# Second layer of a conv/attention hybrid: depthwise sum in PSUM, a scan whose two products add in PSUM, and its side work placed anew

## Chip, cores, metric

The kernel runs on one core of a Trainium2 chip. The metric is device time in microseconds of one whole execution (four layers). All arithmetic is float32, a few small products in float32r.

## What is computed

Only the second layer (L1) is touched. For each of 4 images (128 channels, 64x64) it does a 1x1 product, a depthwise 3x3 convolution with SiLU, a product down to 32 features, and two Mamba-2 scans over the 4096 positions, one forward and one backward; then a batch norm and a gate.

```python
def _mamba2(u, W_in, conv_w, conv_b, dt_bias, A_log, D, norm_w, W_out):
    zxbcdt = u @ W_in
    z, xBC, dt = ...                       # 64, 64+64+64, 1 columns
    xBC = silu(causal_dwconv1d(xBC, conv_w, conv_b))
    xs, Bm, Cm = ...                       # 64 columns each
    dt = softplus(dt + dt_bias)
    dA = exp(dt * -exp(A_log))
    def step(h, inp):
        h = dA_t * h + dtx_t[..., None] * B_t[:, None, :]
        return h, einsum('bhpn,bn->bhp', h, C_t)
    y = (scan of step) + D * xh
    y = y * silu(z)
    y = y * rsqrt(mean(y * y, -1) + 1e-05) * norm_w
    return y @ W_out

o = einsum('bihw,io->bohw', x, lin1_w) + lin1_b
o = silu(depthwise3x3(o, dw_w) + dw_b)
s = o @ fc_in_w
y1, y2 = _mamba2(s, ...[0]), flip(_mamba2(flip(s), ...[1]))
o = batchnorm((y1 + y2) @ fc_out_w)
x = sigmoid(conv4(o)) * x + x
```

## The kernel before, in words

`layer1` (L1007) splits each image's 4096 positions into 8 **groups** of 4 **tiles** of 128 positions; 32 groups in all. The forward and the backward scan go side by side (`dr` 0 and 1). Within a tile the scan is a product of matrices: a masked matrix of decays times C·B (`pairs`, `weigh`, `within`), plus C times the state that came into the tile (`update`).

The main loop (L1485) runs over G, and each group has four **slots** j = 0 to 3. A slot does a piece of several groups at once, in an order written out by hand: the object `InOrder` (L74) makes every engine's instructions stand in program order, so an engine's queue is what the loop says. In the slots of G stand

- for group G: `update` (PE: new state into CY columns 256:320, C times state into 128:192; then DVE: `hst` = state · decay + CY), `weigh` (DVE: `lmc` = `lm` · CY), `within` (PE: `lmc` times x into CY 192:256), `pairs` of the next tile (PE: C·B into CY 0:128), `gated` of the tile before (DVE: two scalings `y` by `ecs`, a sum with the `within` part; POOL: product with the gate into Y);
- for G+1: `spans` (POOL: `ta`), `silus` (ACT), `masks` (PE `psseg`, ACT exp into `lm`), `inputs` (POOL `xw`, DVE `xdt`), `turn_b` (PE `psb`, DVE copy into B), `skips` (ACT);
- for G+2: `project_c` (PE `psc`), `silu_c` (ACT), `lengths` (ACT and eleven small DVE operations), `sums` (PE `pscs`, DVE), `decays` (ACT, POOL);
- for G+3: `project` (PE `pstm` from S4), `take` (DVE: `tm`, `u`);
- for the group 12 ahead (`now`): the nine steps of the convolution, step 0 on ACT and steps 1 to 8 on DVE (L1144), two in each slot; one further ahead (`nxt`) `lines` (PE `pslin`, ACT `lp`); one behind (`last`) `conv_silu` (ACT) and `features` (PE `pss`, four ACT copies into the shifted rows of S4);
- `behind` (L1402): normalisation and output of groups that are done, a generator advanced one step per slot.

The convolution runs for G up to 19, that is in 20 groups that also scan; G = 20 to 31 scan alone. CY is two PSUM tiles of two banks each, used in turn by j. Four further banks (`mm`) serve all other products in turn.

Of the kernel before, what the change touches and what calls it, by code (L numbers as in the profile page):

```python
# [8 lines left out]
F32 = mybir.dt.float32  # L9
# [85 lines left out]
class Kernel:  # L95
# [911 lines left out]
    def layer1(self, after):  # L1007
# [13 lines left out]
        with ExitStack() as ctx:  # L1021
# [23 lines left out]
            def weights():  # L1045
                ps = mm("psw2")
                nc.tensor.matmul(ps[:, 0:P], out_wT, fc_out, start=True, stop=True)
                nc.vector.tensor_scalar(w2, ps[:, 0:P], self.col("norm_w"), None, ALU.mult)
                taps = gp.tile([P, 2, 192], F32, name="taps", tag="C", bufs=3)
                nc.sync.dma_start(taps, self.ins["taps4"])  # L1050
                nc.vector.tensor_mul(wx[:, :, 0:192], wx[:, :, 0:192], taps)
# [6 lines left out]
            nA = cp.tile([P, 2], F32, name="nA")  # L1058

            def constants():  # L1060
# [11 lines left out]
                nc.vector.tensor_copy(ident_r, self.ident)  # L1072
                nc.scalar.activation(nA, self.row("A_log"), AF.Exp)
                nc.vector.tensor_scalar(nA, nA, -1.0, None, ALU.mult)
# [6 lines left out]
            CY = [pp.tile([P, 2, 512], F32, name=f"CY{k}") for k in range(2)]  # L1081
# [53 lines left out]
            def conv(n, b, k):  # L1135
                lp = lps[n, b]
                if k == 0:
                    own = space(n, b)
                    co = own[1] if own else gp.tile([P, 8, HW], F32, name="co")
                    cos[n, b] = co  # L1140
                    nc.scalar.activation(co, lp[:, 0:8, 0:HW], AF.Copy, scale=dw[:, 0:1])
                    return
                co = cos[n, b]
                nc.vector.scalar_tensor_tensor(  # L1144
                    co, lp[:, k // 3:k // 3 + 8, k % 3:k % 3 + HW], dw[:, k:k + 1], co, ALU.mult, ALU.add)
# [10 lines left out]
            def conv_silu(n, b):  # L1156
                src = cos[n, b]
                if len(src.shape) == 2:
                    src = src.rearrange("p (r c) -> p r c", c=HW)
                    own = space(n, b)  # L1160
                    cos[n, b] = own[1] if own else gp.tile([P, 8, HW], F32, name="co")
                nc.scalar.activation(cos[n, b], src, AF.Silu, bias=self.col("dw_b"))

            def features(n, b, moved=False):

                s = S4[n % 2]
                if b == 0:
                    nc.gpsimd.memset(s[:, 0:3], 0.0)
                    nc.gpsimd.memset(s[:, L:L + 3], 0.0)
                ps = mm("pss")  # L1170
                nc.tensor.matmul(ps, fc_in4, cos[n, b].rearrange("p r c -> p (r c)"), start=True, stop=True)
                if moved:
                    nc.scalar.copy(cos[n, b].rearrange("p r c -> p (r c)"), ps)
                for m in range(4):
                    ms = slice(32 * m, 32 * m + 32)
                    if moved:
                        plain.sync.dma_start(s[ms, b * 512 + m:b * 512 + m + 512],
                                             cos[n, b][ms].rearrange("p r c -> p (r c)"))
                    else:
                        nc.scalar.copy(s[ms, b * 512 + m:b * 512 + m + 512], ps[ms, :])  # L1180
# [49 lines left out]
            def silu_c(g):  # L1230
                q = groups[g]
                q.C = gp.tile([P, 512], F32, name="C", bufs=3)
                nc.scalar.activation(q.C, q.pc, AF.Silu, bias=self.col("cb_C"))

            def turn_b(g):
# [5 lines left out]
                nc.vector.tensor_copy(q.B, ps)  # L1241
# [3 lines left out]
            def small(name):  # L1245
                return sp.tile(sh, F32, name=name, bufs=4)

            def lengths(g):
# [3 lines left out]
                u, e, w, lg = q.u, small("e"), small("w"), small("lg")  # L1252
# [16 lines left out]
                q.parts = small("lead"), small("rest")  # L1269
# [4 lines left out]
            def spans(g, dr):  # L1274
                q = groups[g]
                full = [P, GS, P]
                q.ta = []
                for part in q.parts:
# [3 lines left out]
                    q.ta.append(ta)  # L1282

            def sums(g):
# [8 lines left out]
                q.cs = small("cs")  # L1293
                q.tot, q.wd = small("tot"), small("wd")
# [5 lines left out]
            def decays(g):  # L1300
                q = groups[g]
                q.ecs = small("ecs")
                q.et = sp.tile([P, GS], F32, name="et", bufs=4)
                nc.scalar.activation(q.ecs, q.cs, AF.Exp)
# [23 lines left out]
            def masks(g, dr):  # L1328
# [5 lines left out]
                for k, ta in enumerate(q.ta):  # L1334
# [8 lines left out]
            def block(q, dr, j):  # L1343
                b = j if dr == 0 else GS - 1 - j
                return q.C[64 * dr:64 * dr + 64, b * P:(b + 1) * P]

            def pairs(g, j):
                q = groups[g]
                for dr in range(2):
                    nc.tensor.matmul(CY[j % 2][:, dr, 0:P], q.B[64 * dr:64 * dr + 64, j * P:(j + 1) * P],  # L1350
                                     block(q, dr, j), start=True, stop=True)
# [3 lines left out]
            def weigh(g, j):  # L1355
                q = groups[g]
                lm = kp.tile([P, 2, P], F32, name="lmc")
                nc.vector.tensor_tensor(lm, q.lm[:, :, j, :], CY[j % 2][:, :, 0:P], ALU.mult)
                weighted[g, j] = lm

            def update(g, j):
# [5 lines left out]
                cy = CY[j % 2]  # L1367
                for dr in range(2):
                    nc.tensor.matmul(cy[64 * dr:64 * dr + 64, 0, 256:320],
                                     q.tm[:, j, 128 + 64 * dr:192 + 64 * dr], q.xw[:, j, dr, :],  # L1370
                                     start=True, stop=True)
# [4 lines left out]
                nc.vector.scalar_tensor_tensor(h2, state[0], q.et[:, j:j + 1], cy[:, 0, 256:320],  # L1376
# [3 lines left out]
            def within(g, j):  # L1380
                q = groups[g]
                lm = weighted.pop((g, j))
                for dr in range(2):
                    nc.tensor.matmul(CY[j % 2][:, dr, 192:256], lm[:, dr, :], q.xdt[:, j, dr, :],
                                     start=True, stop=True)

            def gated(g, j):
                q = groups[g]
                n, i = divmod(g, NG)
                r, cy = GS * i + j, CY[j % 2]  # L1390
# [92 lines left out]
            for x in left[0:2]:  # L1483
                features(*x, True)
            for G in range(NG + 1 - AHEAD, N + 1):  # L1485
# [9 lines left out]
                if G >= 1 and i >= NG // 2:  # L1495
                    backs.append(behind(n, NG - 1 - i))
                if later:
                    dts = lengths(G + 2)

                for j in range(GS):  # L1500
                    if now is not None and j == 0:
                        conv(*now, 0)
                    if later and j == 0:
                        project_c(G + 2)
# [3 lines left out]
                    if later and j == 0:  # L1508
                        silu_c(G + 2)
                    if last is not None and j == 0:  # L1510
                        conv_silu(*last)
                    if j == 0 and (later or soon or here):
                        nc.scalar.preload_act_table_set("natural_log_exp_and_others")
                    if here:
                        if j == 0 and G == 0:
                            pairs(0, 0)
                        update(G, j)
                        weigh(G, j)
                    if 0 <= G - 1 < N and j == 0:
                        gated(G - 1, GS - 1)  # L1520
                    if here and j:
                        gated(G, j - 1)
                    if first:
                        project(G + 3, j)
                    if soon and j == 1:
                        masks(G + 1, 0)
                        spans(G + 1, 1)
                        inputs(G + 1)
                        turn_b(G + 1)
                    if soon and j == 2:  # L1530
                        masks(G + 1, 1)
                        skips(G + 1)
# [15 lines left out]
                    if nxt is not None and j == 1:  # L1548
                        lines(*nxt)
                    if last is not None and j == 2:  # L1550
# [3 lines left out]
                    for b in list(backs):  # L1554
# [1346 lines left out]
```

## Time and profile before

| | us |
|---|---|
| median of 3 runs | 4900.45 (4896.83 to 4912.55) |
| the profiled execution | 4906.88 |
| its span, first to last instruction | 4904.8 |
| busy in the span: PE / DVE / ACT / POOL | 4487.7 / 3588.3 / 3608.9 / 3064.4 |
| first and last update of the state (`hst`) | 916.1 and 1587.9 |
| update at j = 0 of group 20 | 1386.2 |

The profile writes `DVE` for VectorE, `ACT` for ScalarE, `POOL` for GpSimd, `PE` and `PEld` for TensorE's products and weight loads, `SPq` for the SyncE queue that issues DMAs. A group line reads: line, engine, operation, out<-in, shape, count, busy us, mean ns of one, idle time before and what ended it. Nearly all lines say L85, the helper that records every operation, so tiles' names tell the operations apart. In a windows line the last columns are the granted TensorE clock (1.00 is full speed), the DMA share and GB/s. A float32 product appears as two passes, so counts of PE lines are twice the program's.

### The profile page before, as it was taken

The page shows a single profiled execution, that of the slowest core. Times are in us where ns is not written, and L with a number is a line of the kernel's source. Part 1 is how long each engine was busy: PE and PEld are TensorE (multiplying, and loading weights), DVE is VectorE, ACT ScalarE, POOL GpSimd, SP SyncE. Part 2 cuts the span into 40 slices and gives each one's busy share as a digit, 9 for nine tenths or more (in the row PEclk, how much of TensorE's full clock was granted, in tenths as well). Part 3 has the DMA queues.
Part 4 walks back from the last instruction along what each step waited for, and adds up shares of the span by engine and source line. Part 5 has one row for each costly group of instructions (what it writes and reads, how often), then busy time and mean ns, then how long its engine had stood idle before and what let it go on. Part 6 is the DMA issues. An engine that isn't in the chain of part 4 may idle for free. (4 is left out here: it accounts for less than half of the span.)

```text
span 4904.8 us, 65981 instructions
## 1 busy us (share of the span) xinstructions
PE 4487.7 (91%) x22552; PEld 2439.1 (50%) x22552; DVE 3588.3 (73%) x7198; ACT 3608.9 (74%) x5496; POOL 3064.4 (62%) x3043
## 2 busy tenths in 40 slices
PE   6889977888999699997997999999999999999798
PEld 4777765566666344443443444444444444444344
DVE  5999996788876788874775666666666666665675
ACT  4466644555554677775766999999999999999575
POOL 0334443355555345552797888888888888877488
PEclk9999998788788899998999999999999999999899
DMA  6667772000000300000000000000000000000000
GB/s 211 182 187 187 199 185 67 12 9 10 18 12 16 96 5 1 1 1 0 18 35 18 1 1 1 1 1 1 1 1 1 1 1 1 1 1 1 8 28 35
DMA packets 67474, 190.47 MB, mean 39 GB/s; under 512 B 12532, under 2 KB 15796, under 8 KB 65460
## 3 DMA queue, kind: packets, MB, share of 16 engines
q1 hardware_dynamic: 61700, 170.19, 12.2%
q0 software_dynamic: 2240, 12.85, 0.9%
q8 instruction: 182, 2.98, 0.3%
q10 hardware_dynamic: 3184, 3.08, 0.2%
q14 instruction: 168, 1.38, 0.1%
HBM read 133.23 MB, written 50.74 MB: 38 GB/s over the span
## 5 line engine op out<-in xcount | busy, mean ns | idle before, releaser
L85 POOL TENSOR_TENSOR r<-r 128x512 f32<-128x512 f32 (+1 forms) x1088 | 1349.1, 1241 | 331.6 <-DVE r L85 271.4
L85 DVE TENSOR_TENSOR r<-r,num 128x1024 f32<-128x1024 f32 (+1 forms) x1088 | 974.8, 927 | 597.5 <-PE num L85 502.6
L85 PE MATMUL D<-F,G 32*128 32x512 f32 (+3 forms) x4608 | 1139.9, 573 | 1.8 <-DVE den L85 0.9
L85 PE MATMUL num<-F,G 32*128 32x512 f32 (+3 forms) x4608 | 1057.1, 590 | 6.8 <-DVE r L85 3.9
L85 ACT ACTIVATE r<-r 128x2048 f32<-128x2048 f32 (+4 forms) x610 | 1018.6, 1679 | 51.4 <-POOL r L85 4.3
L85 ACT ACTIVATE r<-D 128x1536 f32<-128x1536 f32 (+1 forms) x544 | 763.4, 1403 | 49.6 <-PE D L85 29.3
L85 PEld LDWEIGHTS D<-F,G 32*128 32x128 f32 x4608 | 484.8, 184 | 372.8 <-issue 235.2
L85 PE MATMUL acc<-r,v 128*128 128x512 f32 (+3 forms) x1152 | 598.1, 606 | 0.7 <-ACT r L85 0.7
L85 POOL TENSOR_TENSOR x<-x 128x512 f32<-128x512 f32 (+2 forms) x320 | 405.4, 1267 | 148.5 <-DVE m L85 66.3
L85 PEld LDWEIGHTS num<-F,G 32*128 32x128 f32 x4608 | 383.4, 183 | 223.4 <-issue 111.4
L85 PE MATMUL pff<-hid,w_ffn_w2T 128*128 128x512 f32 x1024 | 468.0, 600 | 0.0
L85 PE MATMUL pex<-w_expert_w,vT 128*128 128x512 f32 x1024 | 462.6, 600 | 1.6 <-DVE x L85 1.4
L85 POOL TENSOR_TENSOR piece<-v,wt 128x512 f32<-128x512 f32 x160 | 167.5, 1064 | 373.3 <-DVE cum L85 91.7
L85 PEld LDWEIGHTS acc<-r,v 128*128 128x128 f32 x1152 | 174.1, 188 | 382.7 <-issue 188.9
L85 PE MATMUL acc<-ident,pr 128*128 128x128 f32 x2560 | 322.0, 284 | 42.0 <-DVE pr L85 42.0
L85 ACT ACTIVATE x<-pex,gate 128x128 f32<-128x128 f32 x896 | 256.6, 367 | 104.0 <-PE pex L85 78.8
L85 PEld LDWEIGHTS acc<-ident,pr 128*128 128x128 f32 x2560 | 299.2, 147 | 55.8 <-DVE pr L85 54.1
L85 ACT ACTIVATE hid<-phh,cols 128x512 f32<-128x512 f32 x416 | 252.8, 688 | 67.1 <-PE phh L85 67.0
L85 PEld LDWEIGHTS pex<-w_expert_w,vT 128*128 128x128 f32 x1024 | 191.2, 193 | 217.2 <-issue 160.7
L85 PEld LDWEIGHTS pff<-hid,w_ffn_w2T 128*128 128x128 f32 x1024 | 184.9, 190 | 200.6 <-issue 200.6
L85 DVE TENSOR_TENSOR pr<-v,near_w 128x2560 f32<-128x2560 f32 x96 | 270.0, 2813 | 5.6 <-PE acc L85 4.8
L85 POOL TENSOR_TENSOR Y<-y,tm 128x64 f32<-128x64 f32 x256 | 111.7, 456 | 236.3 <-DVE y L85 149.2
(495 smaller groups left out, 7916.4 us busy)
## 6 DMA issues: line engine op xcount, KB each, us to landing
v<-tab SPq DMA_DIRECT2D x320, 256.0 KB
oms<-omw SPq DMA_DIRECT2D x32, 432.0 KB
omr<-oms SPq DMA_DIRECT2D x32, 432.0 KB
X<-in_x_dram SPq DMA_DIRECT2D x8, 1024.0 KB
tab<-vb SPq DMA_DIRECT2D x64, 128.0 KB
o<-o SPq DMA_DIRECT2D x32, 256.0 KB
oin<-o SPq DMA_DIRECT2D x32, 256.0 KB
kept<-X SPq DMA_DIRECT2D x4, 2048.0 KB
```

The costliest lines, as they stand in the source:

```text
L85: self.last = op(*args, **kwargs)
```

## The change

- The convolution's running sum stands in PSUM (`cop`), not in SBUF (`co`), outside the prologue; `conv_silu` writes it to an SBUF tile `co` that has one buffer.
- `features` copies `pss` once into `co` and sends it to S4's four shifted rows by four DMAs (this was the way of the prologue); the two last features of the prologue go by copies, two on ACT and two on DVE.
- `decay` (new): two products per direction with `half_r` give the decay to each position, ACT takes exp, POOL multiplies C by it (`Ce`). The states' product then uses `Ce`, and it and `within` add in the same PSUM columns; `gated` loses its two scalings. `ecs` is gone.
- CY is one tile of two banks; tiles j even and odd use two halves of each bank. `project_c` makes C in tile order, in eight products of 128 columns.
- The copy into B goes from DVE to ACT.
- Slots: `weigh` ahead of `update`, `gated` ahead of both; `silu_c` one group later; `project_c`, `lines`, `skips`, `features` in slot 3; the convolution's steps 3, 2, 1, 2 per slot; up to G = 27 one generator of `behind` advances per slot, not all.

```diff
             def conv(n, b, k):
-                    co = own[1] if own else gp.tile([P, 8, HW], F32, name="co")
+                    co = own[1] if own else pp.tile([P, 512], F32, name="cop").rearrange(
+                        "p (r c) -> p r c", c=HW)
...
             def conv_silu(n, b):
+                    cos[n, b] = gp.tile([P, 8, HW], F32, name="co", bufs=1)
...
-            def features(n, b, moved=False):
+            def features(n, b, moved=True):
...
-                nc.tensor.matmul(q.pc[0:64, :], wx[:, 0, 0:64], s4(g, 0, 0, 512), start=True, stop=True)
-                nc.tensor.matmul(q.pc[64:128, :], wx[:, 1, 0:64], s4(g, 1, GS - 1, 512), start=True, stop=True)
+                for j in range(GS):
+                    for dr in range(2):
+                        nc.tensor.matmul(q.pc[64 * dr:64 * dr + 64, j * P:(j + 1) * P], wx[:, dr, 0:64],
+                                         s4(g, dr, j), start=True, stop=True, skip_group_check=True)
...
-                nc.vector.tensor_copy(q.B, ps)
+                nc.scalar.copy(q.B, ps)
...
+            def decay(g, dr):
+                q = groups[g]
+                if dr == 0:
+                    q.pr = pp.tile([P, 512], F32, name="psrow")
+                for k, ta in enumerate(q.ta[dr]):
+                    nc.tensor.matmul(q.pr, half_r[:, 64 - 64 * dr:192 - 64 * dr], ta.rearrange("p j t -> p (j t)"),
+                                     start=(dr == 0 and k == 0), stop=(dr == 1 and k == 1))
+                if dr == 1:
+                    q.Ce = gp.tile([P, 512], F32, name="Ce")
+                    nc.scalar.activation(q.Ce, q.pr, AF.Exp)
+                    nc.gpsimd.tensor_tensor(q.Ce, q.Ce, q.C, ALU.mult)
...
             def update(g, j):
-                    nc.tensor.matmul(cy[:, dr, 128:192], block(q, dr, j), state[0][64 * dr:64 * dr + 64, :],
-                                     start=True, stop=True)
+                    nc.tensor.matmul(CY[:, dr, at(j, 128, 192)], block(q.Ce, dr, j),
+                                     state[0][64 * dr:64 * dr + 64, :],
+                                     start=False, stop=False, skip_group_check=True)
...
             def within(g, j):
-                    nc.tensor.matmul(CY[j % 2][:, dr, 192:256], lm[:, dr, :], q.xdt[:, j, dr, :],
-                                     start=True, stop=True)
+                    nc.tensor.matmul(CY[:, dr, at(j, 128, 192)], lm[:, dr, :], q.xdt[:, j, dr, :],
+                                     start=False, stop=True, skip_group_check=True)
...
             def gated(g, j):
-                for dr in range(2):
-                    nc.vector.scalar_tensor_tensor(y[:, dr, :], cy[:, dr, 128:192], q.ecs[:, j, dr:dr + 1],
-                                                   q.tm[:, j, 64 * dr:64 * dr + 64], ALU.mult, ALU.add)
-                nc.vector.tensor_tensor(y, y, cy[:, :, 192:256], ALU.add)
+                nc.vector.tensor_tensor(y, q.tm[:, j, 0:128].rearrange("p (d e) -> p d e", d=2),
+                                        CY[:, :, at(j, 128, 192)], ALU.add)
...
                 for j in range(GS):
+                    if last is not None and j == 0:
+                        conv_silu(*last)
                     if now is not None and j == 0:
                         conv(*now, 0)
...
                     if here:
+                        weigh(G, j)
+                        update(G, j)
...
-                    if now is not None:
-                        for k in ((1, 2), (3, 4), (5, 6), (7, 8))[j]:
-                            conv(*now, k)
+                    steps = ((1, 2, 3), (4, 5), (6,), (7, 8))[j] if now is not None else ()
...
-                    if last is not None and j == 2:
+                    if last is not None and j == (2 if last[1] == NG - 1 else 3):
                         features(*last)
...
-                    for b in list(backs):
+                    for b in backs[0:1] if one_by_one else list(backs):
```

More of the change, by code (lines that the diff above doesn't have):

```diff
@@ L1048, in weights @@
                 nc.vector.tensor_scalar(w2, ps[:, 0:P], self.col("norm_w"), None, ALU.mult)
-                taps = gp.tile([P, 2, 192], F32, name="taps", tag="C", bufs=3)
+                taps = gp.tile([P, 2, 192], F32, name="taps", tag="C")
                 nc.sync.dma_start(taps, self.ins["taps4"])
@@ L1058, in layer1 @@
             nA = cp.tile([P, 2], F32, name="nA")
+            half_r = cp.tile([P, 192], F32R, name="half_r")
             def constants():
@@ L1072, in constants @@
                 nc.vector.tensor_copy(ident_r, self.ident)
+                for k in range(3):
+                    nc.vector.tensor_scalar(half_r[:, 64 * k:64 * k + 64], late[:, 0, 0:64], 0.0,
+                                            1.0 if k == 1 else 0.0, ALU.mult, ALU.add)
                 nc.scalar.activation(nA, self.row("A_log"), AF.Exp)
@@ L1078, in layer1 @@
             Y = cp.tile([P, NT + 2 * GS, 2, DI], F32, name="Y")
-            CY = [pp.tile([P, 2, 512], F32, name=f"CY{k}") for k in range(2)]
+            CY = pp.tile([P, 2, 512], F32, name="CY")
             kept = [dram.tile([P, 512], F32, name=f"o{k}") for k in range(NB * NG)]
@@ L1157, in conv_silu @@
                 src = cos[n, b]
+                own = space(n, b)
                 if len(src.shape) == 2:
                     src = src.rearrange("p (r c) -> p r c", c=HW)
-                    own = space(n, b)
-                    cos[n, b] = own[1] if own else gp.tile([P, 8, HW], F32, name="co")
+                if own:
+                    cos[n, b] = own[1]
+                elif (n, b) == (0, 5):
+                    cos[n, b] = gp.tile([P, 512], F32, name="Ce").rearrange("p (r c) -> p r c", c=HW)
+                else:
+                    cos[n, b] = gp.tile([P, 8, HW], F32, name="co", bufs=1)
                 nc.scalar.activation(cos[n, b], src, AF.Silu, bias=self.col("dw_b"))
-            def features(n, b, moved=False):
+            def features(n, b, moved=True):
                 s = S4[n % 2]
@@ L1178, in features @@
                                              cos[n, b][ms].rearrange("p r c -> p (r c)"))
+                    elif m < 2:
+                        nc.scalar.copy(s[ms, b * 512 + m:b * 512 + m + 512], ps[ms, :])
                     else:
-                        nc.scalar.copy(s[ms, b * 512 + m:b * 512 + m + 512], ps[ms, :])
+                        nc.vector.tensor_copy(s[ms, b * 512 + m:b * 512 + m + 512], ps[ms, :])
             def s4(g, dr, j, w=P):
@@ L1231, in silu_c @@
                 q = groups[g]
-                q.C = gp.tile([P, 512], F32, name="C", bufs=3)
+                q.C = gp.tile([P, 512], F32, name="C")
                 nc.scalar.activation(q.C, q.pc, AF.Silu, bias=self.col("cb_C"))
@@ L1240, in turn_b, with small @@
                 q.B = gp.tile([P, 512], F32, name="B")
-                nc.vector.tensor_copy(q.B, ps)
-            def small(name):
-                return sp.tile(sh, F32, name=name, bufs=4)
+                nc.scalar.copy(q.B, ps)
+            def small(name, bufs=4):
+                return sp.tile(sh, F32, name=name, bufs=bufs)
             def lengths(g):
                 q = groups[g]
-                u, e, w, lg = q.u, small("e"), small("w"), small("lg")
+                u, e, w, lg = q.u, small("e", 2), small("w", 2), small("lg", 2)
                 nc.scalar.activation(e, u, AF.Abs)
@@ L1267, in lengths @@
                 nc.vector.tensor_mul(a, dt, nA.unsqueeze(1).to_broadcast(sh))
-                q.parts = small("lead"), small("rest")
+                q.parts = small("lead", 2), small("rest", 2)
                 nc.vector.tensor_copy(q.parts[0].bitcast(F32R), a)
@@ L1276, in spans @@
                 full = [P, GS, P]
-                q.ta = []
+                if dr == 0:
+                    q.ta = [], []
                 for part in q.parts:
@@ L1281, in spans @@
                                             part[:, :, dr].unsqueeze(2).to_broadcast(full), ALU.mult)
-                    q.ta.append(ta)
+                    q.ta[dr].append(ta)
             def sums(g):
@@ L1292, in sums @@
                                  start=True, stop=True)
-                q.cs = small("cs")
-                q.tot, q.wd = small("tot"), small("wd")
+                q.cs = small("cs", 2)
+                q.tot, q.wd = small("tot", 2), small("wd", 2)
                 nc.vector.tensor_copy(q.cs, ps[:, 0:8].rearrange("p (d j) -> p j d", d=2))
@@ L1301, in decays @@
                 q = groups[g]
-                q.ecs = small("ecs")
                 q.et = sp.tile([P, GS], F32, name="et", bufs=4)
-                nc.scalar.activation(q.ecs, q.cs, AF.Exp)
                 nc.scalar.activation(q.wd, q.wd, AF.Exp)
@@ L1333, in masks @@
                 ps = mm("psseg")
-                for k, ta in enumerate(q.ta):
+                for k, ta in enumerate(q.ta[dr]):
                     nc.tensor.matmul(ps, later_r[:, dr, :], ta.rearrange("p j t -> p (j t)"),
@@ L1339, in masks, with block, at @@
                 nc.scalar.activation(q.lm[:, dr].rearrange("p j t -> p (j t)"), ps, AF.Exp)
-            def block(q, dr, j):
-                b = j if dr == 0 else GS - 1 - j
-                return q.C[64 * dr:64 * dr + 64, b * P:(b + 1) * P]
+            def decay(g, dr):
+                q = groups[g]
+                if dr == 0:
+                    q.pr = pp.tile([P, 512], F32, name="psrow")
+                for k, ta in enumerate(q.ta[dr]):
+                    nc.tensor.matmul(q.pr, half_r[:, 64 - 64 * dr:192 - 64 * dr], ta.rearrange("p j t -> p (j t)"),
[4 more added lines that the diff above has]
+                    nc.gpsimd.tensor_tensor(q.Ce, q.Ce, q.C, ALU.mult)
+            def block(c, dr, j):
+                return c[64 * dr:64 * dr + 64, j * P:(j + 1) * P]
+            def at(j, lo, hi):
+                return slice(256 * (j % 2) + lo, 256 * (j % 2) + hi)
             def pairs(g, j):
@@ L1349, in pairs @@
                 for dr in range(2):
-                    nc.tensor.matmul(CY[j % 2][:, dr, 0:P], q.B[64 * dr:64 * dr + 64, j * P:(j + 1) * P],
-                                     block(q, dr, j), start=True, stop=True)
+                    nc.tensor.matmul(CY[:, dr, at(j, 0, P)], block(q.B, dr, j), block(q.C, dr, j),
+                                     start=True, stop=True, skip_group_check=True)
             state, weighted, outs = {}, {}, {}
@@ L1357, in weigh @@
                 lm = kp.tile([P, 2, P], F32, name="lmc")
-                nc.vector.tensor_tensor(lm, q.lm[:, :, j, :], CY[j % 2][:, :, 0:P], ALU.mult)
+                nc.vector.tensor_tensor(lm, q.lm[:, :, j, :], CY[:, :, at(j, 0, P)], ALU.mult)
                 weighted[g, j] = lm
@@ L1366, in update @@
                     nc.vector.memset(state[0], 0.0)
-                cy = CY[j % 2]
                 for dr in range(2):
-                    nc.tensor.matmul(cy[64 * dr:64 * dr + 64, 0, 256:320],
+                    nc.tensor.matmul(CY[64 * dr:64 * dr + 64, 0, at(j, 192, 256)],
                                      q.tm[:, j, 128 + 64 * dr:192 + 64 * dr], q.xw[:, j, dr, :],
-                                     start=True, stop=True)
+                                     start=False, stop=True, skip_group_check=True)
                 for dr in range(2):
-                    nc.tensor.matmul(cy[:, dr, 128:192], block(q, dr, j), state[0][64 * dr:64 * dr + 64, :],
-                                     start=True, stop=True)
+                    nc.tensor.matmul(CY[:, dr, at(j, 128, 192)], block(q.Ce, dr, j),
+                                     state[0][64 * dr:64 * dr + 64, :],
+                                     start=False, stop=False, skip_group_check=True)
                 h2 = kp.tile([P, DI], F32, name="hst", bufs=3)
-                nc.vector.scalar_tensor_tensor(h2, state[0], q.et[:, j:j + 1], cy[:, 0, 256:320],
+                nc.vector.scalar_tensor_tensor(h2, state[0], q.et[:, j:j + 1], CY[:, 0, at(j, 192, 256)],
                                                ALU.mult, ALU.add)
@@ L1383, in within @@
                 for dr in range(2):
-                    nc.tensor.matmul(CY[j % 2][:, dr, 192:256], lm[:, dr, :], q.xdt[:, j, dr, :],
-                                     start=True, stop=True)
+                    nc.tensor.matmul(CY[:, dr, at(j, 128, 192)], lm[:, dr, :], q.xdt[:, j, dr, :],
+                                     start=False, stop=True, skip_group_check=True)
             def gated(g, j):
@@ L1389, in gated @@
                 n, i = divmod(g, NG)
-                r, cy = GS * i + j, CY[j % 2]
+                r = GS * i + j
                 y = kp.tile([P, 2, DI], F32, name="y")
-                for dr in range(2):
-                    nc.vector.scalar_tensor_tensor(y[:, dr, :], cy[:, dr, 128:192], q.ecs[:, j, dr:dr + 1],
-                                                   q.tm[:, j, 64 * dr:64 * dr + 64], ALU.mult, ALU.add)
-                nc.vector.tensor_tensor(y, y, cy[:, :, 192:256], ALU.add)
+                nc.vector.tensor_tensor(y, q.tm[:, j, 0:128].rearrange("p (d e) -> p d e", d=2),
+                                        CY[:, :, at(j, 128, 192)], ALU.add)
                 for dr in range(2):
@@ L1483, in layer1 @@
             for x in left[0:2]:
-                features(*x, True)
+                features(*x, False)
             for G in range(NG + 1 - AHEAD, N + 1):
@@ L1496, in layer1 @@
                     backs.append(behind(n, NG - 1 - i))
+                one_by_one = G < N - NG // 2
                 if later:
@@ L1500, in layer1 @@
                 for j in range(GS):
+                    if last is not None and j == 0:
+                        conv_silu(*last)
                     if now is not None and j == 0:
                         conv(*now, 0)
-                    if later and j == 0:
-                        project_c(G + 2)
                     if soon and j == 0:
@@ L1507, in layer1 @@
                         silus(G + 1)
[L1508 to L1511, printed above, removed]
+                        silu_c(G + 1)
                     if j == 0 and (later or soon or here):
                         nc.scalar.preload_act_table_set("natural_log_exp_and_others")
[L1514 to L1518, printed above, removed]
+                    if here and j == 0 and G == 0:
+                        pairs(0, 0)
                     if 0 <= G - 1 < N and j == 0:
@@ L1522, in layer1 @@
                         gated(G, j - 1)
+                    if here:
+                        weigh(G, j)
+                        update(G, j)
                     if first:
@@ L1526, in layer1 @@
                         masks(G + 1, 0)
+                        decay(G + 1, 0)
                         spans(G + 1, 1)
@@ L1531, in layer1 @@
                         masks(G + 1, 1)
-                        skips(G + 1)
+                        decay(G + 1, 1)
                     if later and j in (1, 2):
@@ L1542, in layer1 @@
                             pairs(G + 1, 0)
-                    if now is not None:
-                        for k in ((1, 2), (3, 4), (5, 6), (7, 8))[j]:
-                            conv(*now, k)
+                    steps = ((1, 2, 3), (4, 5), (6,), (7, 8))[j] if now is not None else ()
+                    for k in steps[:1]:
+                        conv(*now, k)
                     if first:
                         take(G + 3, j)
-                    if nxt is not None and j == 1:
+                    for k in steps[1:]:
+                        conv(*now, k)
+                    if soon and j == 3:
+                        skips(G + 1)
+                    if later and j == 3:
+                        project_c(G + 2)
+                    if nxt is not None and j == 3:
                         lines(*nxt)
-                    if last is not None and j == 2:
+                    if last is not None and j == (2 if last[1] == NG - 1 else 3):
                         features(*last)
```

## Prediction

> **What bounds the kernel now.** The change is confined to the second layer. I read first the windows view over that layer's main loop, split where the depthwise convolution ends (columns: stretch, length, then busy time of PE, PEld, DVE, ACT, POOL, the granted PE clock, DMA share, GB/s).
>
> ```profile
> 916.00:1386.00 470.00, 417.48 (x2180) 288.34 (x2178) 404.33 (x1091) 263.73 (x490) 244.81 (x374) 0.79 0.03 10
> 1386.00:1604.00 218.00, 196.53 (x1206) 141.84 (x1204) 146.13 (x521) 107.18 (x209) 120.63 (x193) 0.85 0.05 18
> ```
>
> The first stretch is 20 groups (G = 0 to 19) with a convolution beside them: 23.5 us each, VectorE (DVE) busy for 20.2 of it. The second is 12 groups and what follows them; from the updates of `hst`, groups 20 to 28 take 150 us (16.7 each) and no engine but PE is near full there. So first DVE, then PE. The groups view of the first stretch (busy, mean ns, then idle before) and the tile view of `co` tell what DVE does:
>
> ```profile
> L85 DVE SCALAR_TENSOR_TENSOR co<-lp,cols,co 128x512 f32<-128x512 f32 x160 | 163.3, 1020 | 2.8
> L85 ACT COPY S<-pss 32x512 f32<-32x512 f32 x80 | 46.1, 577 | 69.8 <-PE pss L85 69.1
> L85 DVE SCALAR_TENSOR_TENSOR y<-CY,ecs,tm 128x64 f32<-128x64 f32 x158 | 36.9, 273 | 0.0
> L85 DVE COPY B<-psb 128x512 f32<-128x512 f32 x20 | 13.6, 682 | 4.8 <-PE psb L85 4.8
> L85 DVE SCALAR_TENSOR_TENSOR co<-lp,cols,co x192: 739/752/1610, 852.5 to 1382.8; 128x512 f32<-128x512 f32 x192
> ```
>
> A convolution step takes 0.752 us alone and up to 1.61 us beside POOL's products; the mean is 1.02. `lmc` (0.411) and `y`, which read one operand from PSUM, do not stretch beside POOL. The waits view of the same stretch shows that PE waits on DVE, and DVE seldom on PE:
>
> ```profile
> PEld CY L85 <- DVE lmc L85: 59.6, 33, 3.9
> DVE hst L85 <- PE CY L85: 26.8, 24, 2.7
> ```
>
> **What is removed.** Per convolution group on DVE: eight `y` scalings (0.46 per pair in the timeline, 1.84), the copy of B (0.68, now ACT's), and the stretching of eight convolution steps whose sum now stands in PSUM (8 x 0.27 = 2.1): 4.6 of 20.2 us. No row shows DVE writing PSUM; the copy of B out of PSUM (0.682) and `xdt` with both inputs in SBUF (0.755 with stretching) bound a step between 0.68 and 1.02, and I take 0.752, the same step undisturbed. ACT loses three of four 0.577 copies of `pss` and one small exponential, and gains B (0.6) and the exponential for `Ce` (0.6, as `lm`); POOL gains one product (1.04, as `ta`). Neither is near full (263.7 and 244.8 of 470), so these are free unless they stand in a chain. PE gains four `psrow` products (0.23 apart at full clock, as `psseg`: 0.9) and `psc` in 128-column pieces: 0.9 now; four pieces like `CY<-C,B` at 0.49 would be 2.0; I take 1.4, between.
>
> [...]
>
> **What is put on the path: features by DMA.** In the steady loop `features` now copies `pss` into `co` and sends it to S by four DMAs on SP. `co` has one buffer. The waits of the built program say that the next group's first ACT work, the table load before `conv_silu`, waits for all four DMAs (they read `co`), and behind it on ACT stand `conv_silu`, the convolution's step 0, `silus` and `silu_c`. DVE's step 1 waits for step 0, and everything later on DVE for step 1. The prologue shows what such a send costs:
>
> ```profile
> L1177 SPq DMA_DIRECT2D S<-tm x24: 507/588/609, 850.2 to 877.4; - x24
> ```
>
> ```profile
> 859.38 0.64 ACT L85 ACTIVATE tm<-pslin,cols 128x448 f32<-128x448 f32 x1 [1.73 <-DMA S<-tm]
> ```
>
> The tile view of `S` gives the issues (min/median/max ns), ACT's timeline the wait. Issues are 0.63 apart; one issued at 857.16 released ACT at 859.23, 2.05 later. Four cost 3 x 0.63 + 2.05 + 0.07 = 4.0 us from the copy's end. SP carries besides these only the stores of `o`, whose copies stand earlier on ACT, so the four wait for nothing there. `psc` and `lines` are moved into slot 3 too, ahead of `pss` on PE.
>
> **What is put on the path: one CY.** States and pairs now share two banks, and in the built program PE's update(j) waits for DVE's `lmc`(j), DVE's `hst`(j) for that update, `within`(j) for `hst`(j), and `y`(j) for pairs(j+1). Before, update(j) ran ahead of `lmc`(j). So DVE, in order, idles in each slot while PE makes the update:
>
> ```profile
> 1172.37 0.34 PE L85 MATMUL CY<-xw,tm 128*64 128x64 f32 x4
> 1172.64 0.44 PE L85 MATMUL CY<-hst,C 64*128 64x64 f32 x4
> 1173.00 0.92 PE L85 MATMUL pstm<-w_in_w,S 128*128 128x193 f32 x4
> 1173.63 0.77 PE L85 MATMUL psseg<-ta,later_r 128*128 128x512 f32 x2
> ```
>
> 0.71 plus signals: 0.85 us at full clock, 1.4 at half.
>
> **The new loop of a convolution group,** from the end of `lmc`(3), at full clock. PE: update 0.8, `pstm` 0.63, sums 0.5, within 0.55, pairs 0.5, `psc` 1.4, `pslin` 0.9, `pss` 1.0: 6.3. ACT copy 0.65: 6.95. DMAs 4.0: 10.95. Table load 1.28, `conv_silu` 0.7, step 0 0.7: 13.6. DVE is ready for step 1 at about 7.2 (cs, steps 7 and 8, take, y, lmc, and hst after PE's `pss`), so it stands 6.4 us. Then DVE: steps 1 to 3 and take 2.9; y, lmc 0.63; update wait and `hst` 1.15; `xdt` 0.7; then `w` waits for ACT's `e`, which now stands behind the copy of B (PE's pstm, psseg, psrow, psb from the same lmc 3.0, copy 0.75, two `e` 0.45): 2.5; `w` 0.3; steps 4, 5 and take 2.1; slot 2: 0.63 + 1.15 + lengths 2.14 + step 6 and take 1.33; y, lmc 0.63. Sum 16.1; the loop is 29.7 us.
>
> PE is idle for some 8 us of it, from pairs(1) at 8.7 to `lmc`(1) at 17. What idling does to the clock, before:
>
> ```profile
> 1246.00:1250.00 4.00, 1.21 (x7) 0.73 (x5) 4.00 (x8) 1.53 (x4) 1.39 (x4) 1.00 0.02 9
> 1250.00:1264.00 14.00, 13.81 (x50) 8.79 (x50) 8.95 (x32) 6.12 (x15) 6.31 (x9) 0.51 0.09 35
> ```
>
> After under 3 us idle the clock is half for 13.7 us, though PE is busy. At half clock slot 1 of the new loop grows by 2.8 us: 32.5. I take 31, between, as slots 2 and 3 may fall either way.
>
> [...]
>
> **The sum.** 18 groups x (31 - 23.5) = +135. Groups 5 and 13 follow a group whose `features` stands one slot earlier; without the DMA wait the loop is 29.7 - 6.4 = 23.3, as before: 0. The same wait in group -1: +6; in group 20, on `silus` alone: +3. Groups 20 to 28: every slot is now PE's update to pairs (2.3, 3.9, 3.5 and 2.8 us at full clock, with masks, `psrow`, `psb` and sums where they stand) and then 0.85 of y, lmc and signals on DVE: 15.9; `psc` outlasts that cover by 0.6 and back work by 0.5: 17.0 x 9 = 153 against 150: +3. Back work, spread one step a slot, falls mostly into DVE's stall: 0. The last two features of the prologue no longer go by DMA (PE waited 5.8 for one): -4. Total +143 on the profiled 4906.9 (span 4904.8): 5050. That execution is 6.4 above the median of the runs shown; on the median's footing **5043 us**.
>
> **Rivals.**
> 1. *DVE stays the bound and the DMA wait is hidden* (faster). If step 0 ends on ACT within 7.2 us of `lmc`(3), DVE never stands, and each group loses 4.6, less 1 for the handoffs that remain: 20 x -3.6 = -72, 4830 us. For it: DVE is 86% busy, and ACT is idle 44%. Against it: the copy, four issues, landing, table load, silu and step 0 alone are 7.35 after `pss`.
> 2. *Half hidden*: PE reaches `pss` earlier or the clock stays full, loop 26: 18 x 2.5 + 10 = +55, 4955.
> 3. *Half clock throughout* (slot 3 too, +4): loop 35, +217, 5120.
> 4. *PSUM does not end the stretching* (the change does not do what it says): steps stay at 1.02; six of them lie in the loop: 18 x 1.6 = +29 on the forecast, 5075, inside its own range.
>
> **Chances.** Forecast with 4 (4990 to 5110): 0.60. Rival 2 (4920 to 4990): 0.17. Rival 3: 0.08. Rival 1: 0.10. Within 0.3%, about what a measurement of this kernel can tell from no change, by a near balance of gains and stalls: 0.05. So faster 0.10, same 0.05, slower 0.85. The range leaves out rival 1, the balance and the far end of 3: 4930 to 5125.
>
> **What would show it.** Convolution steps at 0.75 in every case (else 4). `conv_silu` idle before, released by DMA S<-co, about 4 us in 18 groups; DVE idle before step 1 about 6 us, released by ACT; DVE idle before `hst` 0.8 to 1.4 in every slot, released by PE; groups of about 31 us between updates at j = 0; a PE clock under 0.79 in that stretch; groups 5 and 13 shorter than their neighbours. If DVE's idle before step 1 is under 2 us, the forecast is wrong and rival 1 is what happens.

## The result, and the profile after

The changed kernel takes 5211.71 us (median of 4 runs, 5202.77 to 5217.24) against 4902.66 on the same chip: ratio 1.0626, 95% interval 1.0603 to 1.065, 309 us slower. The forecast was 5043 us, +143, with a range up to 5125: the direction was right, the size was not, and the time lies outside the range. The profiled execution is that of 5202.77 us, its span 5201.1.

The windows view of the second layer's loop, cut again where the convolution ends (stretch, length, busy time of PE, PEld, DVE, ACT, POOL, granted PE clock, DMA share, GB/s):

```profile
927.00:1628.00 701.00, 469.87 (x2498) 363.09 (x2496) 304.30 (x914) 248.18 (x449) 217.76 (x396) 0.72 0.05 14
1628.00:1823.00 195.00, 162.18 (x1098) 131.79 (x1098) 90.09 (x342) 92.65 (x172) 96.05 (x152) 0.86 0.04 15
```

The 20 convolution groups take 701 us and not 470, though DVE is busy for 304 and not 404: its work fell by 5 us a group as forecast, and no engine is full any more. The clock fell from 0.79 to 0.72. So the time is in waits and in the lower clock. The waits view of that stretch (engine, what waits, for whom: total us, times, longest), first DVE's, then ACT's and PE's:

```profile
DVE hst L85 <- PE CY L85: 117.1, 80, 5.4
DVE cop L85 <- ACT cop L85: 112.4, 20, 6.5
DVE w L85 <- ACT e L85: 88.6, 20, 4.6
DVE cs L85 <- PE pscs L85: 27.1, 20, 2.4
DVE y L85 <- PE CY L85: 23.4, 16, 1.9
...
ACT L85 <- DMA S<-co: 57.4, 18, 3.6
...
PE CY L85 <- DVE lmc L85: 230.0, 61, 9.6
```

The three large waits of DVE are `hst` for PE's update, convolution step 1 for ACT's step 0, and `w` for ACT's `e`. Behind the second stands the DMA wait, in 18 groups as forecast. The last row is the largest wait of PE's products: 230 us of standing ahead of the update, until DVE has made `lmc`. The timeline of PE from group 1 shows what stands in its queue then:

```profile
962.05 0.55 PE L85 MATMUL CY<-xdt,lmc 128*128 128x64 f32 x4
962.53 0.49 PE L85 MATMUL CY<-C,B 64*128 64x128 f32 x4
971.43 0.48 PE L85 MATMUL CY<-xw,tm 128*64 128x64 f32 x4 [8.41 <-DVE lmc L85]
971.85 0.69 PE L85 MATMUL CY<-hst,Ce 64*128 64x64 f32 x4
972.47 1.65 PE L85 MATMUL pstm<-w_in_w,S 128*128 128x193 f32 x4
973.67 1.31 PE L85 MATMUL psseg<-ta,later_r 128*128 128x512 f32 x2
974.77 0.63 PE L85 MATMUL psseg<-never,ident_r 128*128 128x512 f32 x1
975.20 1.05 PE L85 MATMUL psrow<-ta,half_r 128*128 128x512 f32 x2
976.05 0.69 PE L85 MATMUL psb<-ident,tm 128*128 128x128 f32 x4
```

PE is done with the pairs at 963.0 and stands until 971.4; then come the update, 0.48 + 0.69 and not 0.34 + 0.44 us (half clock; the granted clock is 0.60 from 971.4 to 977.5), and behind it `pstm`, `psseg`, `psrow` and `psb`, in which nothing needs `lmc`. DVE in the same stretch (start, length, idle before and its end):

```profile
961.41 0.28 DVE L85 SCALAR_TENSOR_TENSOR hst<-hst,et,CY 128x64 f32<-128x64 f32 x1 [3.32 <-PE CY L85]
968.12 0.75 DVE L85 SCALAR_TENSOR_TENSOR cop<-lp,cols,cop 128x512 f32<-128x512 f32 x1 [6.43 <-ACT cop L85]
...
972.59 0.28 DVE L85 SCALAR_TENSOR_TENSOR hst<-hst,et,CY 128x64 f32<-128x64 f32 x1 [1.21 <-PE CY L85]
972.79 0.69 DVE L85 TENSOR_TENSOR xdt<-tm,dt 128x512 f32<-128x512 f32 x1
977.75 0.30 DVE L85 TENSOR_SCALAR w<-e 128x8 f32<-128x8 f32 x1 [4.28 <-ACT e L85]
```

It stands 6.43 us before step 1 (forecast 6.4), 1.21 before `hst`, 4.28 before `w`. From one update at j = 0 to the next:

| stretch | before | after | difference | forecast |
|---|---|---|---|---|
| up to the first update | 916.1 | 927.1 | +11 | +2 |
| 18 convolution groups | 420.1 | 637.0 | +217 | +135 |
| groups 5 and 13 | 50.0 | 64.3 | +14 | 0 |
| groups 20 to 28 | 150.4 | 194.6 | +44 | +6 |
| rest of the loop | 51.3 | 60.9 | +10 | 0 |

Together +296, all of the difference of the spans.

### The profile page after: what moved, and what is told of

The parts are those of the page before. It is cut to its first block, busy times and chain, and to the rows that moved or that the text cites. A ratio compares the mean times of both kernels' runs of the same rounds, so it can differ in the third digit from the quotient of the medians.

```text
span 5201.1 us, 67084 instructions
## 1 busy us (share of the span) xinstructions
PE 4566.2 (88%) x23064; PEld 2545.2 (49%) x23064; DVE 3458.6 (66%) x6917; ACT 3606.4 (69%) x5458; POOL 3049.4 (59%) x3075
## 5 line engine op out<-in xcount | busy, mean ns | idle before, releaser
L85 ACT ACTIVATE r<-r 128x2048 f32<-128x2048 f32 (+4 forms) x610 | 1019.5, 1681 | 51.3 <-POOL r L85 4.3
L85 PE MATMUL CY<-xw,tm 128*64 128x64 f32 x512 | 50.1, 282 | 275.5 <-DVE lmc L85 274.7
```

The source lines that it names most:

```text
L85: self.last = op(*args, **kwargs)
```

## Experiments

Theory: the changed kernel pays for three waits (the features' DMA, the update behind `lmc`, `w` behind the copy of B), and more than forecast because PE's standing brings more of the half clock (0.72 granted in the convolution stretch, 0.79 before). Rivals: the DMA wait alone decides; or the chain of hand-offs would take this long at any clock. Each kernel's excess is its median less that of the kernel before on the same chip (4894 to 4903), beside the ratio's 95% interval; a group is the mean of groups 0 to 19, and of 20 to 28, in the profiled execution.

| kernel | excess us | interval | group 0-19 | 20-28 |
|---|---|---|---|---|
| before | 0 | | 23.5 | 16.7 |
| after | +309 | 1.0603-1.065 | 35.1 | 21.6 |
| warm | +255 | 1.0495-1.054 | 31.7 | 23.5 |
| split | +316 | 1.061-1.0659 | 34.7 | 23.1 |
| upd | +102 | 1.0182-1.0232 | 26.2 | 18.1 |
| early | +224 | 1.043-1.0475 | 30.4 | 22.4 |
| f2 | +230 | 1.0456-1.0491 | 31.1 | 22.4 |
| uf | +30 | 1.0048-1.0088 | 23.3 | 18.6 |
| uef | +17 | 1.002-1.0044 | 23.1 | 17.3 |
| ef | +140 | 1.0267-1.0303 | 27.1 | 21.3 |
| allb | +332 | 1.0652-1.0693 | 35.8 | 23.0 |
| warm_tail | +316 | 1.0632-1.0667 | 34.7 | 22.5 |
| upd_tail | +281 | 1.055-1.0585 | 35.3 | 19.2 |
| b_cop | -43 | 0.9881-0.9918 | 20.6 | 16.7 |
| b_cop_dma | -51 | 0.988-0.9914 | 19.9 | 16.7 |
| b_cop_dmaB | -49 | 0.9882-0.9928 | 20.6 | 16.5 |

**warm: fill PE's standing**

```diff
+                    for _ in range((7, 2, 0, 0)[j] if now is not None and here else 0):
+                        w_ = mm('warm') if _ == 0 else w_
+                        nc.tensor.matmul(w_, fc_in4, lps[now][:, 0:8, 0:HW], start=True, stop=True)
```

> The changed kernel with matmuls that nobody reads, put in front of the waiting update: seven of 128x512 after the products of slot 0 and two after those of slot 1, in the 8.4 and 2.9 us in which PE stands there (group 1 of the changed kernel). Theory A, the half clock that follows PE's standing makes the loop 35 and not 31 us: slots 1 to 3 run at full clock, w waits 2.5 and not 4.3 us, y(3) 0 and not 1.8, psc to pss 3 and not 4.3, so a group is some 4 to 5 us shorter, 20 x -4 = -80, about 5125 us, and the granted clock of the convolution stretch rises from 0.72 to above 0.9. Theory B, the loop is long by its chain of hand-offs and the clock is a by-product: the clock rises and the time stays within 15 us of the changed kernel, or grows by what the extra matmuls delay.

The result is 54 us less than the changed kernel. The stretch's row and the place of the fill:

```profile
927.00:1560.00 633.00, 540.12 (x2856) 357.73 (x2856) 302.36 (x914) 245.98 (x449) 217.41 (x396) 0.93 0.06 15
```

```profile
959.45 6.28 PE L85 MATMUL warm<-lp,w_fc_in 128*128 128x512 f32 x14
969.04 0.34 PE L85 MATMUL CY<-xw,tm 128*64 128x64 f32 x4 [3.31 <-DVE lmc L85]
```

PE still stands 3.31 us there, but the clock rose from 0.72 to 0.93 and the convolution stretch lost 68 us, 3.4 a group: theory A, at two thirds of its -80 in the median and with 3.4 instead of 4 to 5 us a group. Groups 20 to 28, which the edit leaves alone, took 17 us more; why is not known (in `split` and `f2` they took 14 and 7 more). The run also shows what is, at 0.93, not the clock: 31.7 us a group are left.

**split: features without DMA, but with copies on DVE**

```diff
-            def features(n, b, moved=True):
+            def features(n, b, moved=False):
```

> The changed kernel with the features copied from PSUM to S in four copies of 32 rows (two on ACT, two on DVE) and no DMA. Theory A, the DMA wait is on the path: ACT's table load stands 3.6 us less, conv_silu starts 1.2 us after pss and not 4.6, DVE stands 3.0 and not 6.4 us before step 1, so 18 groups lose 3.4 us each: -61, about 5140 us; shorter standing may save some clock too, at most another 20. Theory B, the chain that sets the loop runs elsewhere (PE's update, then w) and step 1 has slack: within 15 us of the changed kernel.

Nothing gained, but not for theory B's reason: the edit made a new wait. DVE's two copies stand ahead of `y` and `lmc` in its queue and wait for ACT's:

```profile
992.53 1.40 DVE L85 COPY S<-pss 32x512 f32<-32x512 f32 x2 [5.97 <-ACT S L85]
993.96 0.29 DVE L85 TENSOR_TENSOR y<-tm,CY 128x128 f32<-128x128 f32 x1
```

Step 1 no longer waits in group 1, `lmc` does. This run tells nothing of the DMA's price; f2 does.

**upd: the update ahead of y and lmc**

```diff
+                    if here:
+                        update(G, j)
                     if 0 <= G - 1 < N and j == 0:
                         gated(G - 1, GS - 1)
...
                         weigh(G, j)
-                        update(G, j)
```

> The changed kernel with update(j) ahead of y(j-1) and lmc(j) in every slot, so that PE makes it right after pairs(j). Theory A, the hand-off lmc to update to hst is what costs: DVE's 117 us before hst in the convolution stretch and 37 in groups 20 to 28 fall to a third, and PE's 230 us of waiting for lmc shrink with them: -60 to -110 us, about 5110, a convolution group near 31, groups 20 to 28 near 19 us instead of 21.6. Theory B, the same PE time is waited for one instruction later, at lmc or y: less than 20 us gained.

It took 207 us off, twice theory A's upper end. The timeline of PE in group 1 shows the update right after the pairs, and the slot's other products behind it, while DVE still waits for step 0:

```profile
950.68 0.49 PE L85 MATMUL CY<-C,B 64*128 64x128 f32 x4
951.10 0.34 PE L85 MATMUL CY<-xw,tm 128*64 128x64 f32 x4
951.36 0.44 PE L85 MATMUL CY<-hst,Ce 64*128 64x64 f32 x4
```

The waits on DVE in 926 to 1448, the convolution groups:

```profile
DVE cop L85 <- ACT cop L85: 107.2, 20, 6.0
DVE hst L85 <- PE CY L85: 58.5, 32, 6.3
DVE w L85 <- ACT e L85: 15.7, 18, 1.7
```

`hst`'s wait fell to half, not to a third, and `w`'s from 88.6 to 15.7 us although the copy of B still stands ahead of `e`: most of it was PE's queue behind the update. The wait for step 0 stayed.

**early: e and lg ahead of the masks and the copy of B**

```diff
+                    if later and j in (1, 2):
+                        next(dts)
                     if soon and j == 1:
                         masks(G + 1, 0)
...
-                    if later and j in (1, 2):
-                        next(dts)
```

> The changed kernel with the exponentials e and lg of the lengths ahead of the masks' exponential and the copy of B on ACT. Theory A, w behind the copy of B is on the path (88.6 us of DVE standing in the convolution stretch, 4.3 a group): w no longer waits, convolution steps 4 and 5 and lmc(2) come up to 2 to 4 us sooner, 20 x -2 to -4, about 5140 us. Theory B, pairs(2) on PE come no sooner, since they stand behind psseg, psrow and psb at half clock, so DVE waits at y instead: less than 20 us gained.

It took 85 us off; `w` has no row left among DVE's waits, and the clock of the stretch is 0.81. So a wait that the forecast had as 2.5 us a group, and did not doubt, was worth 4.

**f2, uf, uef, ef: the three waits together and apart**

```diff
-                    if last is not None and j == (2 if last[1] == NG - 1 else 3):
+                    if last is not None and j == 2:
                         features(*last)
```

> The changed kernel with features (pss, its copy and the four DMAs) in slot 2 of every group and not in slot 3; nothing on DVE moves. Theory A, the DMA wait is on the path by itself: slot 0 is 7.7 us as in groups 5 and 13 of the changed kernel and not 11, 18 groups lose 3.4 us, about -61, 5145 us. Theory B, the time is set by PE's update between lmc and hst with its half clock, and what slot 0 gives back the later slots take (groups 5 and 13 of the changed kernel had slot 0 at 7.7 and still took 35.0 and 29.4): within 20 us of the changed kernel.

f2 took 79 us off, 18 x 3.4 and some more: theory A. Its waits on DVE show the DMA's part gone (112.4 to 53.5 us before step 1) and the others as they were:

```profile
DVE hst L85 <- PE CY L85: 105.7, 81, 4.8
DVE w L85 <- ACT e L85: 84.3, 20, 4.6
DVE cop L85 <- ACT cop L85: 53.5, 20, 3.5
```

The first update stands at 915.9: the 11 us ahead of it were the DMA wait too.

> Update ahead of y and lmc as in upd, and features in slot 2. In upd DVE stands 5.9 us before step 1 in each group (107 us in the stretch), the largest wait left. Theory A, with the hand-off gone the DMA wait is what bounds a convolution group: slot 0 goes from 9.4 to 5.9 us (groups 5 and 13 of upd), 18 x -3.4 = -61, about 4940 us. Theory B, the later slots take it back, as they may in f2: within 20 us of upd (5002).

uf is 72 us below upd, above A's 61.

> As uf, and the exponentials e and lg ahead of the masks' exponential and the copy of B. In upd DVE waits 24 us for e in the convolution stretch and 17 in groups 20 to 28. If they are on the path: another -20 to -40 against uf, about 4910, level with the kernel before. If w's wait was only the form in which PE's half clock showed in the changed kernel (there it cost 88 us), it is nothing here: within 10 us of uf.

uef is 13 us below uf, between the two cases and nearer to the second. (The 24 us of the expectation were read over 926 to 1530, some tail groups with them; in the convolution stretch they are the 15.7 above.) `w` costs 85 us when it is undone first, and 13 when the other two are gone.

> The changed kernel with features in slot 2 and with e and lg early, but with update behind lmc as the change has it: against uef (4912) only the hand-off is left. Theory A, the hand-off costs what the forecast gave it, 0.85 to 1.4 us a slot: 80 + 36 slots, 100 to 160 us, so 5010 to 5070 us. Theory B, all of a slot's PE work queued behind the update starts late, and with it the clock: 200 us or more as between the changed kernel and upd, 5110 or above.

ef is 123 us above uef: theory A, the price that the forecast gave the hand-off. Undone first it was 207. Singly, the three are 207 + 85 + 79 = 371; together 292. The likely reason, which no run isolates, is that each shortens PE's standing and with it the half clock that makes the others dear: the stretch's clock is 0.72 in the changed kernel and 0.78, 0.81 and 0.84 in f2, early and upd.

**warm_tail, upd_tail, allb: the groups without a convolution**

```diff
+                    for _ in range((0, 2, 2, 1)[j] if now is None and here else 0):
+                        w_ = mm('warm') if _ == 0 else w_
+                        nc.tensor.matmul(w_[:, 0:256], fc_in4, X[:, 0:256], start=True, stop=True)
```

> The changed kernel with matmuls that nobody reads (128x256, two after the products of slots 1 and 2, one after those of slot 3) in the groups that have no convolution. Theory A, half clock after PE's standing of 0.6 to 1.5 us a slot is the excess: the clock of groups 20 to 28 goes from 0.86 to near 1, a group from 21.6 towards 17.5, -25 to -35 us in all. Theory B, the order is the excess and the clock adds little: the extra matmuls delay the update by as much as they help, within 10 us of the changed kernel or above it.

```profile
1629.00:1823.00 194.00, 166.99 (x1118) 131.79 (x1116) 90.93 (x333) 85.67 (x166) 91.83 (x145) 0.92 0.04 13
```

The clock rose from 0.86 to 0.92, the groups did not get shorter (22.5 us, within the 21.6 to 23.5 that they took in other runs without an edit there): theory B. This doesn't prove the clock worthless, since the fill can itself delay the update: at 1657.79 the update follows it without a wait:

```profile
1656.73 1.13 PE L85 MATMUL warm<-X,w_fc_in 128*128 128x256 f32 x4
1657.79 0.34 PE L85 MATMUL CY<-xw,tm 128*64 128x64 f32 x4
```

upd_tail has upd's diff where `now is None` alone.

> The changed kernel with update ahead of y and lmc in the groups without a convolution alone; groups before 20 as the change has them. Both theories give about 18.1 us a group there, as in upd (163 us for groups 20 to 28 against 195): -30 to -35, and some 6 in the last three groups, so about 5170 us. If upd's gain there came from how its convolution groups left the clock and the queues: under -15.

28 us less, 19.2 us a group: the order is about half of the tail's excess (21.6 against 16.7 before).

```diff
-                    for b in backs[0:1] if one_by_one else list(backs):
+                    for b in list(backs):
```

> The changed kernel with all back chains advanced in every slot, as before the change, and not one a slot. The forecast put this part at nothing. Theory A: within 15 us of the changed kernel. Theory B, the spread back work lengthens slots one after the other where DVE and PE wait for each other (groups 20 to 28 took 21.6 and not 17 us): up to -30.

23 us more than the changed kernel, with intervals that just miss each other: neither theory. Spreading the back work is if anything a small gain.

**b_cop, b_cop_dma, b_cop_dmaB: single parts on the kernel before**

```diff
-            pm = ctx.enter_context(tc.tile_pool(name="l1pm", bufs=4, space=PSUM))
+            pm = ctx.enter_context(tc.tile_pool(name="l1pm", bufs=3, space=PSUM))
...
-                    co = own[1] if own else gp.tile([P, 8, HW], F32, name="co")
+                    co = own[1] if own else pp.tile([P, 512], F32, name="cop").rearrange(
+                        "p (r c) -> p r c", c=HW)
```

> The kernel before with one part of the change alone: the convolution's sum stands in one PSUM bank (conv_silu then writes a co in SBUF, and goes ahead of the next group's step 0), and the pool of matmul banks has three instead of four. Theory A, a step takes 0.75 and not 1.02 us, and since DVE is 86% busy there the group loses most of 8 x 0.27 = 2.1 us: 20 x -1 to -2.1, 4860 to 4880 us. Theory B, steps are shorter but the shorter ring of banks or the order conv_silu before step 0 makes DVE or PE wait as long: within 10 us of the kernel before, or above it.

Faster than both kernels, than the kernel before by 0.8 to 1.2%. A step costs 0.752 us on the mean and not 1.020, beside the same POOL products, with one bank fewer:

```profile
L85 DVE SCALAR_TENSOR_TENSOR cop<-lp,cols,cop 128x512 f32<-128x512 f32 x160 | 120.3, 752 | 5.8 <-ACT cop L85 3.0
```

b_cop_dma adds `def features(n, b, moved=True)`; b_cop_dmaB also `nc.scalar.copy(q.B, ps)`.

> The kernel before with the sum in PSUM (b_cop), and its features sent by one copy and four DMAs in slot 2, from a co of two buffers, so that no later write waits for them. In b_cop's group 1 PE stands 0.95 us before pscs until ACT's four copies of pss are done, and from 960.3 to 969.9 PE then runs at half clock, 20.5 us a group against 17.3 in group 10 at full clock. Theory A (half clock from standing): the copy takes 0.59 and not 2.3 us, the 0.95 goes, the clock of the stretch rises from 0.87 to above 0.93, and the groups near 20.5 go towards 17.5: -20 to -40 against b_cop, about 4820 us. Theory B (the DMA's 4 us are a price wherever they stand): psc and the projections wait for S, 18 x 1 to 3 us more than b_cop, above 4870.

The clock rose from 0.87 (920 to 1332) to 0.92 (918 to 1320) and the stretch fell from 412 to 397 us in the profiled executions, but the medians (4853.1 and 4847.05) can't be told apart. What is settled is that theory B is wrong: the same four DMAs, with a second buffer and a slot's distance, cost nothing that can be measured.

> As b_cop_dma, and the copy of B on ACT as in the change. If DVE bounds b_cop_dma, 20 x up to 0.68 off: some -10 against it. If PE bounds it, or w behind the copy of B on ACT stops DVE as in the changed kernel (there 4.3 us a group): the same or up to +40.

No difference from b_cop_dma that can be measured.

## Why the forecast was right in direction and short in size

- **Convolution steps 0.752 in PSUM:** right; 0.741 to 0.757, mean 0.749. DVE's work fell by 5.0 us a group (forecast 4.6). Rival 4 is out. The shortest step is 0.739 us with the sum in SBUF and 0.741 with it in PSUM.
- **Features by DMA:** the mechanism and its size were right: 3.97 us from the copy's end to the table load in group 1 (4.0), DVE's stand 6.43 (6.4). Undone, it gave 79 us.
- **Half clock: the step that failed.** "At half clock slot 1 of the new loop grows by 2.8 us: 32.5. I take 31". In group 1 most products from the update at 971.4 to 987 take the half clock's times (0.63 granted), and again `psc` and most of `pslin` (0.70 from 990.8 to 995): `w` waits 4.28 us (2.5), the `y` ahead of `lmc`(3) 1.77 (0), `psc` to `pss` are 4.2 us (3.3). That is rival 3's loop, 35, given 0.08. `warm` sizes the term: the clock is worth about 3.4 us a group (35.1 less 31.7), and the sum took 1.3 (31 less the 29.7 at full clock). Cut at the updates of `hst`, the computed 29.7 has slots 0 to 3 of 11.1, 7.4, 5.3 and 6.0 us; the 18 groups took 10.9, 9.7, 6.8 and 8.0, and with PE's standing filled 11.1, 8.2, 5.2 and 7.5. So slot 0, with the DMAs, was right, and most of what was missing in slots 1 and 2 is the clock. What keeps slot 3 at 7.5 was not measured.
- **One CY:** 0.85 to 1.4 us a slot held at its place (ef against uef: 123 us in 116 slots, 1.06 each), but "DVE, in order, idles in each slot while PE makes the update" names the update alone. The PE queue behind it enters the sum only ahead of `pss` and of `w`, at full clock. In the changed kernel update and queue together are worth 207 us (upd), 8.9 us in a convolution group (35.1 to 26.2).
- **Groups 5 and 13: 0.** Wrong: they took 35.0 and 29.4 us. "29.7 - 6.4" takes off DVE's whole stand before step 1, but only the DMA's 3.4 go: slot 0 is 7.7 us and not 4.7, and DVE still waits for ACT's step 0. Half clock and hand-off remain as well.

```profile
1106.15 0.75 DVE L85 SCALAR_TENSOR_TENSOR cop<-lp,cols,cop 128x512 f32<-128x512 f32 x1 [2.99 <-ACT cop L85]
```

- **Groups 20 to 28 at 17.0.** Wrong: 21.6. Only group 28, at clock 1.00, has 17.2. upd_tail gives back 2.4 a group, uef 4.3. How the rest divides between clock, back work and `w` was not measured.
- **What the gain came to:** uef, with the three waits undone, has 16.5 us of DVE work a group and still takes 23.1. PE is busy for 414.6 of 463 us at clock 0.87 (row below), and DVE still stands 54.6 us before `hst` and 48.8 before step 1. b_cop, which adds no PE work, takes 20.6. So the convolution's sum in PSUM pays, alone. That the decays on C move work from DVE to PE, which then bounds, is likely, but they and the single CY were not run alone.

```profile
916.00:1379.00 463.00, 414.56 (x2503) 297.78 (x2504) 330.08 (x914) 242.73 (x452) 226.68 (x397) 0.87 0.07 21
```

- **Slips in the working** that move nothing: rival 4 is 5072 (5043 + 29), rival 3 +215 and 5115 (18 x 4 more); no row shows a release at 859.23, ACT starts at 859.38.

## What to carry to other kernels

When an instruction on an in-order engine is put behind a wait, price the whole queue behind it until the next point that others wait for, and not the instruction alone (here update and queue were worth 207 us). Where PE then stands, cost the stretch after it at half clock as a likely case, not as the far end (here 0.60 was granted for 6.1 us after a stand of 8.41 us, and 0.51 for 14 us after one of 2.98 in the kernel before). When several waits end in one loop, undo them in more than one order: theirs did not add here (371 singly, 292 together).

## What the runs showed of the hardware

The low clock came with stands of under 1 us. In b_cop PE stands 0.95 us in each of these periods of some 20 us (at 956.7 and 977.1), and between them is busy for 10.00 of 10 us at 0.51 (windows view, columns as above):

```profile
940.00:950.00 10.00, 10.00 (x49) 8.54 (x45) 6.76 (x20) 5.98 (x10) 5.10 (x8) 0.51 0.00 0
950.00:960.00 10.00, 9.05 (x59) 6.09 (x59) 9.19 (x34) 5.66 (x13) 2.79 (x10) 1.00 0.01 2
960.00:970.00 10.00, 10.00 (x47) 8.37 (x43) 6.75 (x21) 6.26 (x9) 5.10 (x9) 0.51 0.00 0
970.00:980.00 10.00, 9.05 (x59) 6.30 (x61) 9.30 (x34) 5.43 (x14) 3.00 (x11) 0.98 0.00 0
1145.00:1163.30 18.30, 16.88 (x112) 11.78 (x113) 17.59 (x58) 12.22 (x23) 8.20 (x17) 1.00 0.00 1
```

The last row follows a like stand of 0.95 us, which ends at 1145.05 in the same kernel: 18.3 us at 1.00. What decides between the two was not found.
